# A graph layer on one core: turns of one pair of blocks instead of two, sums that lag, and a gate for every unit's gathers

## The chip, the core and the metric

One Trainium2 chip, one core of it. The core has TensorE (PE in the profile, with its weight loads as PEld), VectorE (DVE), ScalarE (ACT), GpSimd (POOL) and SyncE (SP); each works through its own instructions in order and waits for others by semaphores. DMA transfers are issued from the queues of SP, ACT and POOL. The metric is the device time of one execution in microseconds, as a median over runs.

## What is computed

A layer of a graph network over 6250 nodes of 256 features and 206250 edges, sorted by destination, all in float32. Cut to what matters:

```python
h = jnp.maximum(_layernorm(x), 0.0)
polarity = jnp.clip(edge_attr[:, 0:1], 0.0, 1.0)
raw = edge_attr[:, 1:]                                        # 64 features an edge
e = jax.nn.relu(raw @ W_e1.T + b_e1) @ W_e2.T + b_e2
edge_emb = (e * (polarity + 0.01)) @ W_le.T + b_le
msg = jax.nn.relu(h[src] + edge_emb)
aggr = jax.ops.segment_sum(msg, dst, num_segments=6250)
g = (h + aggr) @ W_g1.T + b_g1
g = layernorm(g) * ln_g + ln_b
out = x + jax.nn.relu(g) @ W_g2.T + b_g2
```

## The kernel before

**Layout of the work.** Edges come in tiles of 128; four tiles are a block (512 edges), half a block (two tiles, 256 edges) is a **unit**, and two blocks, so four units, are a **pair**. There are 403 blocks, 806 units (`NU`) and 202 pairs (`NP`). The two matrices after the first relu are multiplied into one in the prologue (`wc_s`), so an edge passes three stages of matmuls:

- **First layer** (`first_layer`, line 310), per pair: eight matmuls in the profile, 64 rows deep and 512 columns wide, two blocks at a time in the two halves of the array. Each of the four results fills a PSUM bank; three are evicted by ACT (line 327), one by DVE (line 324), with bias and relu, into `e1`. It runs two pairs ahead.
- **Edge products** (`edge_part`, line 347), per unit: eight matmuls of 128 x 128 weights and 256 columns into one bank. DVE evicts it with the bias into `msg` (line 353).
- **Sums** (`add_up`, line 740), per pair: 16 matmuls by a one-hot matrix `sel` of 128 x 32, four of them side by side in the array, which add the messages of a destination into `pd`.

Seven PSUM banks go round (`Ring`) among the first two stages and the node work; `pd` is the eighth. A bank is taken again when its reader, seven takings ago, has read it.

**Gathers and products.** Between the second and the third stage stands `whole(u)`: DVE multiplies `msg` by the polarity and adds the node rows `h[src]` (line 718, two instructions a unit), and ACT takes the relu (line 725). The node rows are fetched by POOL with two indirect DMAs a unit (`gather`, line 663) from `hb_d`, which the prologue writes. POOL has 1604 of these to issue and, from its first one on, nothing else. Their targets are 20 places in SBUF (`HG`), a place being free when the sums of the unit 20 before are done; the profile names the places `hx` and `hg`.

**Order.** The whole order is written out by the main loop over units `u` from `LEAD` = 22 on. Each turn of the loop makes the edge products of unit `u` (`forward`), then as many products `whole(made)` as fall due, then at most one piece of node work (`due`). The number of products due is `u + 1 - lag`, with a lag of 18 units at the start that falls by one every `SHRINK` = 44 units to 1 at the end (lines 978 and 979). So edges run ahead of products by up to 22 units, and the lead is used up over the run.

At `u % 4 == TURN` = 1 `forward` calls `turn_of(q)` for the pair `q = u // 4`. Between pairs `FEW` = 6 and 196 (`by_two`) this acts at even pairs alone, and for two pairs: first the sums of all pairs that are ready (`add_pairs`, line 772: those whose four products have been issued), then the first layers of pairs `q + 2` and `q + 3`, then the loads of raw features on SP. Outside that range it acts at each pair: first layer, then sums, then loads. In the unit before a turn by two, one product is held back until after the turn (the last term of `lag`).

**Gates.** Gathers are issued in step with PE. `paced` (that is `in_step`, line 676) is called behind every edge product and every half of a first layer with the planner's cost of it (`EDGE` 1.754, `LAYER` 0.9; sums add `SUMS` 0.46 a block and node steps `NODES` 0.81), which add up to `spent`. At two places in eight units (`gate`) it issues all gathers for which `(got - 2 * RAW) * STEP < spent + AFLOAT + HALF`, with `STEP` = 1.288 a gather, `AFLOAT` = 6.0 and `HALF` the cost of four units; the first of them waits for the PE instruction just made, the others follow it in POOL's order. A first call ahead of the loop lets the first gathers go without a wait. If a product is due whose gather is not yet issued, `gathers(made + 1)` issues it.

**Node work.** When the last group of sums that reaches a window of 128 nodes is done, `far_work` issues, over the following units, the read of the sums, two transposes (lines 174, 207), and the two products of the node's own layers (lines 189, 220) with their normalisation on DVE and ACT. `due` lets one such step go per unit, none in the unit before a turn by two and in the turn's own (`QUIET`, units 0 and 1 of every eight).

Of the kernel before, what the change touches and what calls it, by code (L numbers as in the profile page):

```python
# [36 lines left out]
NP = -(-NB // 2)  # L37
# [3 lines left out]
LEAD = 22  # L41
LEAST = 1
EDGE, LAYER, SUMS, NODES = 1.754, 0.9, 0.46, 0.81
STEP = 1.288
AFLOAT = 6.0
HALF = 4 * EDGE + 2 * LAYER + 2 * SUMS + NODES
BANKS = 7
SHRINK = 44
RAW = 4
HG = 16 + RAW  # L50
FEW = 6
QUIET = (0, 1)
TURN = 1
# [48 lines left out]
def gnn_kernel(ctx: ExitStack, tc: tile.TileContext, x, src_c, dst_c, dst_r, pol_c, raw_t, w_e1t, w_e2,  # L102
# [138 lines left out]
    NU = 2 * NB  # L241
    fast = ExitStack()
    fast.enter_context(tc.manual_schedule())
    with fast:
# [39 lines left out]
        def load_pair(q):  # L284
            if q >= NP:
                return
            t, k = divmod(q, 2)
            if k == 0:
                fours[t] = ld.tile([P, 2, 512], F32, name="raw")
            raw[q] = fours[t][:, k, :]  # L290
            if q < 4:
                nc.sync.dma_start(out=raw[q], in_=raw_t[t, :, k, :])
            elif k == 0:
                nc.sync.dma_start(out=fours[t], in_=raw_t[t])

        def first_layer(q):

            bs = [b for b in (2 * q, 2 * q + 1) if b < NB]
            if not bs:
                return  # L300
            for b in bs:
                e1[b] = features[b % 8]
            pe, z, readers = {}, {}, {}
            for c in range(2):
                olds = []
                for s, b in enumerate(bs):
                    pe[s, c] = ps().rearrange("p a b -> p (a b)")
                    olds.append(ps.old())
                for s, b in enumerate(bs):
                    z[c] = nc.tensor.matmul(pe[s, c], we1_s[s * F:(s + 1) * F, c * P:(c + 1) * P],  # L310
                                            raw[q][s * F:(s + 1) * F, :], start=True, stop=True)
                    ps.wrote(z[c], len(bs) - 1 - s)
                    reader, writer = olds[s]
                    readers[s, c] = reader
                    if reader is not None and writer is not None:
                        tc.declare_no_dep(z[c].ins, writer.ins, reason="the bank's reader has waited for it")
                    if s == 0:
                        for reader, _ in olds[1:]:
                            behind(z[c], reader)
                paced(LAYER, z[c], c == 0 and not (by_two(q - 2) and q % 2))  # L320
            for c in range(2):
                for s, b in enumerate(bs):
                    if s == c == 1:
                        a = nc.vector.tensor_scalar(e1[b][:, c, :], pe[s, c], be1_s[:, c:c + 1], 0.0, op0=ALU.add,  # L324
                                                    op1=ALU.max)
                    else:
                        a = nc.scalar.activation(e1[b][:, c, :], pe[s, c], AF.Relu, bias=be1_s[:, c:c + 1])  # L327
                    behind(a, z[c])
                    evictions[b, c] = a
                    apart_from(a, evictions.get((b - 8, c)), readers[s, c])  # L330
                    ps.read(a, len(bs) * (1 - c) + len(bs) - 1 - s)
            raw.pop(q)
# [5 lines left out]
        def edge_part(u):  # L338

            nonlocal last_z  # L340
            b, v = divmod(u, 2)
            pz = ps()
            before, _ = ps.old()
            for i in range(2):
                k = (2 * v + i) * P
                for c in range(2):
                    last_z = nc.tensor.matmul(pz[:, i, :], e1[b][:, c, k:k + P], wc_s[:, c, :], start=c == 0, stop=c == 1)  # L347
            ps.wrote(last_z)
            msg[u] = msg_p.tile([P, 2, D], F32, name="msg")
            if plain(u):  # L350
                a = nc.scalar.activation(msg[u], pz, AF.Copy)
            else:
                a = nc.vector.tensor_add(msg[u], pz, bc_s)  # L353
            ps.read(a)
            apart_from(a, before)
            if v == 1:
                e1.pop(b)
            paced(EDGE, last_z, by_two(u // 4) and u % 8 == 5)

        last_z = None  # L360
        sums = lambda last: None
        paced = lambda us, behind, gate=False: None

        def by_two(q):
            return FEW <= q < NP - FEW

        def turn_of(q):


            if not by_two(q):  # L370
                if q + 2 < NP:
                    first_layer(q + 2)
                sums(q == NP - 1)
                if q % 2 == 0:
                    load_pair(q + 4)
                    load_pair(q + 5)
            elif q % 2 == 0:
                sums(False)
                first_layer(q + 2)
                first_layer(q + 3)  # L380
                load_pair(q + 4)
                load_pair(q + 5)

        def forward(u):

            edge_part(u)
            if u % 4 == TURN:
                turn_of(u // 4)

        nc.vector.memset(eps_t, EPS)  # L390
# [42 lines left out]
        with tc.tile_pool(name="p1", bufs=4) as p1, tc.tile_pool(name="p1x", bufs=11) as p1x:  # L433
# [76 lines left out]
            for k in range(len(parts) + 1):  # L510
                last = len(parts) - 1
# [20 lines left out]
                for _ in range((k > 0) + (k > 2 and k % 3 > 0)):  # L532
                    u = next(units, None)
# [108 lines left out]
        with tc.tile_pool(name="hg", bufs=1) as hg_p, tc.tile_pool(name="ms", bufs=4) as ms_p, \  # L642
# [6 lines left out]
            got = 2 * RAW  # L649
            acc = {}  # L650
            done = {}
            made = 0
# [18 lines left out]
            def gathers(last):  # L671

                while got < 2 * min(NU, last):
                    gather()

            def in_step(us, behind, gate=False):

                nonlocal spent
                spent += us
                while gate and (got - 2 * RAW) * STEP < spent + AFLOAT + HALF and got < 2 * min(NU, 4 * summed + HG):  # L680
                    gather(behind)
                    behind = None

            def select(g):

# [86 lines left out]
            def add_pairs(last=False):  # L772

                nonlocal summed
                whole_groups = []
                pairs = 0
                while summed + pairs < NP and min(4 * (summed + pairs) + 4, NU) < made + last:
                    pairs += 1
                for _ in range(pairs):
                    newest = done.get(4 * summed + 3, ())  # L780
                    for b in (2 * summed, 2 * summed + 1):
                        if b < NB:
                            whole_groups.append(add_up(b, newest))
                            newest = ()
                            if b % L == 0 and group_of(b) + 2 < NG:
                                rest.extend(select(group_of(b) + 2))
                    summed += 1

                for g in whole_groups:
                    keep(g)  # L790
# [151 lines left out]
            def due():  # L942

                nonlocal spent
                fns = todo.pop(now, deque())
                if fns and not (by_two(now // 4) and now % 8 in QUIET):
                    spent += NODES
                    fns.popleft()()
                if fns:
                    todo.setdefault(now + 1, deque()).extendleft(reversed(fns))  # L950

            gathers(RAW + 1)
            sums = add_pairs
            paced = in_step
            in_step(0.0, None, True)
            def strips():
                rows_of_edges()
                rest.extend(select(0) + select(1))
# [12 lines left out]
            for u in range(LEAD, NU):  # L971
                now = u
                forward(u)

                if u >= NU - 24:
                    gathers(4 * summed + HG)

                lag = max(LEAST, LEAD - RAW - u // SHRINK) + (by_two(u // 4) and (u + 1) % 8 == TURN)
                ready_for = min(u + 1 - lag, 5 * (u + 1 - LEAD) // 4)
                between = piece  # L980
                while made < ready_for:
                    gathers(made + 1)
                    whole(made, between)
                    made += 1
                    between = lambda: None
                if between is piece:
                    piece()
                due()
                for fn in moves.pop(now, []):
                    fn()  # L990
                if len(rest) > 3:
                    piece()
                if u == NU - 24:
                    for w in range(NW):
                        if groups_of(w)[-1] == NG - 1:
                            late[w] = node_work(w, True)
                if u == LEAD + 60:
                    flag = nc.values_load(bad_i[0:1, 0:1], min_val=0, max_val=4 * P)
# [214 lines left out]
```

## Time and profile before

| | us |
|---|---|
| median of 3 runs | 2155.08 |
| lowest, highest | 2152.94, 2156.09 |
| the profiled execution, its own time | 2150.16 |
| its span from first to last instruction | 2148.4 |

The granted TensorE clock of the profiled execution is 0.996 of full speed. In a row of groups stand: line, engine, operation, tile written and tiles read, count, busy time and mean duration in ns, then the idle time just before these instructions and what ended it. A row of waits has the waiting group, the releaser, the summed wait, how often, and the longest. A row of the chain or of the timeline has start, duration and what ran; the chain is the run's last-ending work followed back, and where PE carries it, its pieces lie end to end. A row of a window has its bounds and length, then busy time and count of PE, PEld, DVE, ACT and POOL, the granted clock, DMA share and GB/s. fp32 matmuls overlap their neighbours, so a matmul's mean duration is longer than the distance between two of them.

### The profile page before, as it was taken

What the parts mean: (1) busy time and instruction counts of PE and PEld (TensorE: products, weight loads), DVE (VectorE), ACT (ScalarE), POOL (GpSimd) and SP (SyncE); (2) the same over time, 40 slices, a digit from 0 to 9 for tenths busy, and PEclk for the clock granted to TensorE, in tenths of its full rate; (3) what the DMA queues carried; (4) which work ended last, traced back from release to release, by engine and by line L of the source; (5) the groups of instructions that cost most, each with busy time, mean ns of one, the idle gap of its engine ahead of it and who ended that gap; (6) DMA issues with size and microseconds to landing.
All of it is one profiled execution on the core that took longest, in us unless ns stands there. A gap on an engine that the chain in (4) does not pass through costs nothing.

```text
span 2148.4 us, 33462 instructions
## 1 busy us (share of the span) xinstructions
PE 2104.8 (98%) x11940; PEld 1559.8 (73%) x11940; DVE 1594.2 (74%) x3455; ACT 1010.0 (47%) x1804; POOL 1621.4 (75%) x1675
## 2 busy tenths in 40 slices
PE   9999999999999999999999999999999999999998
PEld 6677776777777676777777776777777777777766
DVE  7888776877777777777777767776777777777776
ACT  7544444444444444444444444444544454444443
POOL 6777777777777777777777777777777777777775
PEclk9999999999999999999999999999999999999999
DMA  9544545455545444544454554455444455454543
GB/s 317 185 147 140 152 148 159 142 154 152 163 149 155 148 150 145 162 141 152 144 153 148 160 159 136 147 158 159 144 150 144 149 156 152 148 152 140 160 139 92
DMA packets 143638, 330.35 MB, mean 154 GB/s; under 512 B 35999, under 2 KB 71416, under 8 KB 142712
## 3 DMA queue, kind: packets, MB, share of 16 engines
q0 software_dynamic: 77376, 211.39, 34.2%
q1 hardware_dynamic: 64788, 113.47, 15.9%
q10 hardware_dynamic: 1300, 3.28, 0.4%
q8 instruction: 95, 1.56, 0.3%
q14 instruction: 79, 0.65, 0.1%
HBM read 306.24 MB, written 34.08 MB: 158 GB/s over the span
## 4 chain that ended last, share of the span: by engine, by line
PE 53%; POOL 26%; issue 11%; DMA 6%; DVE 3%; ACT 0%; SPq 0%; POOLq 0%; ACTq 0%; DVEq 0%
PE pz L347 35%; POOL hg L663 21%; PE pz L310 10%; POOL hx L663 5%; PE pd L740 4%; DMA hg<-hb_d,src_s 4%; PE pz L220 1%; DVE hg L718 1%; PE pz L189 1%; DMA raw<-in_raw_t_dram 1%; DVE msg L353 1%; DMA hx<-hb_d,src_s 1%; PE pz L207 0%; DVE st L159 0%; PE pz L174 0%
## 5 line engine op out<-in xcount | busy, mean ns | idle before, releaser
L663 POOL DMA_INDIRECT hg<-hb_d,src_s x1284 | 1259.7, 981 | 393.8 <-issue 368.6
L347 PE MATMUL pz<-wc_s,e 128*128 128x256 f32 x6448 | 1456.0, 382 | 2.1 <-DVE msg L353 2.1
L347 PEld LDWEIGHTS pz<-wc_s,e 128*128 128x128 f32 x6448 | 1212.0, 190 | 238.2 <-ACT e L327 74.1
L725 ACT ACTIVATE hg<-hg 128x512 f32<-128x512 f32 x641 | 404.2, 631 | 806.2 <-DVE hg L718 806.2
L718 DVE SCALAR_TENSOR_TENSOR hg<-msg,pol_s,hg 128x256 f32<-128x256 f32 x1284 | 591.4, 479 | 229.4 <-DMA hg<-hb_d,src_s 225.8
L353 DVE TENSOR_TENSOR msg<-pz,bc_s 128x512 f32<-128x512 f32 x799 | 542.3, 683 | 15.9 <-PE pz L347 15.2
L310 PE MATMUL pz<-raw,we_s 64*128 64x512 f32 x1612 | 384.0, 608 | 18.4 <-DVE msg L353 9.9
L663 POOL DMA_INDIRECT hx<-hb_d,src_s x320 | 316.8, 990 | 97.5 <-issue 92.9
L327 ACT ACTIVATE e<-pz,vecs 128x512 f32<-128x512 f32 x605 | 360.8, 693 | 60.3 <-PE pz L310 59.9
L324 DVE TENSOR_SCALAR e<-pz,vecs 128x512 f32<-128x512 f32 x201 | 150.6, 749 | 206.6 <-PE pz L310 206.2
L310 PEld LDWEIGHTS pz<-raw,we_s 64*128 64x128 f32 x1612 | 145.5, 187 | 211.1 <-issue 130.4
L725 ACT ACTIVATE hx<-hx 128x512 f32<-128x512 f32 x164 | 103.4, 631 | 195.1 <-DVE hx L718 195.1
L718 DVE SCALAR_TENSOR_TENSOR hx<-msg,pol_s,hx 128x256 f32<-128x256 f32 x328 | 151.8, 480 | 57.4 <-DMA hx<-hb_d,src_s 56.7
L740 PE MATMUL pd<-hg,sel 128*32 128x256 f32 x2560 | 160.4, 384 | 11.0 <-ACT hg L725 11.0
L740 PEld LDWEIGHTS pd<-hg,sel 128*32 128x32 f32 x2560 | 74.7, 110 | 82.0 <-issue 25.9
L694 DVE SCALAR_TENSOR_TENSOR sel<-iota_w,zero_c,rel 128x256 f32<-128x256 f32 x202 | 96.5, 478 | 0.0
L189 PE MATMUL pz<-wg_s,hT 128*128 128x256 f32 (+1 forms) x196 | 50.8, 382 | 0.8 <-ACT hT L178 0.8
L220 PE MATMUL pz<-wg_s,nT 128*128 128x256 f32 (+1 forms) x196 | 50.5, 380 | 0.9 <-ACT nT L211 0.9
L740 PE MATMUL pd<-hx,sel 128*32 128x256 f32 x656 | 43.5, 382 | 0.0
L189 PEld LDWEIGHTS pz<-wg_s,hT 128*128 128x128 f32 (+1 forms) x196 | 36.8, 190 | 7.6 <-ACT hT L178 1.2
L470 POOL TENSOR_TENSOR hb<-xt,rows_b 128x256 f32<-128x256 f32 (+1 forms) x49 | 34.1, 727 | 10.5 <-ACT e L327 3.5
L220 PEld LDWEIGHTS pz<-wg_s,nT 128*128 128x128 f32 (+1 forms) x196 | 37.0, 190 | 6.6 <-ACT nT L211 1.1
(113 smaller groups left out, 518.0 us busy)
## 6 DMA issues: line engine op xcount, KB each, us to landing
raw<-in_raw_t_dram SPq DMA_DIRECT2D x99, 512.0 KB
hg<-hb_d,src_s POOLq DMA_INDIRECT x1284
sum_d<-zero_d SPq DMA_DIRECT2D x47, 256.0 KB
ab<-sum_d SPq DMA_DIRECT2D x47, 256.0 KB
sum_d<-ms SPq DMA_DIRECT2D x264, 32.0 KB
hb_d<-hb SPq DMA_DIRECT2D x12, 512.0 KB
xt<-in_x_dram SPq DMA_DIRECT2D x48, 128.0 KB
out_dram<-ot SPq DMA_DIRECT2D x48, 128.0 KB
```

The costliest lines, as they stand in the source:

```text
L189: z = nc.tensor.matmul(ph[:n, 0, :], aT[:, c, :n], wg1_s[:, c, :], start=c == 0 and not bias_by_pe, stop=c == 1)
L220: z = nc.tensor.matmul(po[:n, 0, :], nT[:, c, :n], wg2_s[:, c, :], start=c == 0, stop=c == 1)
L310: z[c] = nc.tensor.matmul(pe[s, c], we1_s[s * F:(s + 1) * F, c * P:(c + 1) * P], raw[q][s * F:(s + 1) * F, :], start=True, stop=True)
L324: a = nc.vector.tensor_scalar(e1[b][:, c, :], pe[s, c], be1_s[:, c:c + 1], 0.0, op0=ALU.add, op1=ALU.max)
L327: a = nc.scalar.activation(e1[b][:, c, :], pe[s, c], AF.Relu, bias=be1_s[:, c:c + 1])
L347: last_z = nc.tensor.matmul(pz[:, i, :], e1[b][:, c, k:k + P], wc_s[:, c, :], start=c == 0, stop=c == 1)
L353: a = nc.vector.tensor_add(msg[u], pz, bc_s)
L663: g = nc.gpsimd.indirect_dma_start(out=hg[u][:, i, :], out_offset=None, in_=hb_d, in_offset=bass.IndirectOffsetOnAxis(ap=src_s[:, 2 * u + ...
L694: nc.vector.scalar_tensor_tensor(sel[g][:, k * S:k * S + n, :], iota_w.rearrange("p (o w) -> p o w", o=1).to_broadcast([P, n, W]), zero_c, ...
L718: product = nc.vector.scalar_tensor_tensor(hg[u][:, i, :], m[:, i, :], pol_s[:, 2 * u + i:2 * u + i + 1], hg[u][:, i, :], op0=ALU.mult, op ...
L725: done[u] = product, nc.scalar.activation(hg[u], hg[u], AF.Relu)
L740: z = nc.tensor.matmul(acc[g][j * W:(j + 1) * W, :], sel[g][:, k * S + j, :], m[:, j % 2, :], start=k == 0, stop=b == blocks_of(g)[-1])
```

## The change

Five things, in the code of one function each:

1. `turn_of`: every pair has its own turn, over the whole run: first layer of pair `q + 2`, then the sums, then the loads at even pairs. The hold-back of a product in the unit before a turn goes with it, from every eighth unit to every fourth.
2. `add_pairs`: a pair is summed only when its last unit lies `LATER` = 3 units further behind the products issued (not at the end of the run), and the product made early in the turn does not count.
3. `forward` calls `ahead` (`one_ahead`) before the turn: one product, with its relu, is issued ahead of the turn's first layer, and so ahead of its evictions on DVE and ACT.
4. `in_step`: every call is a gate, for one unit (two gathers) at most, of which the first waits for the PE instruction; `HALF` is gone from the condition, and so is the call that let the first gathers go ahead of the loop.
5. `due`: node steps keep out of units 0 and 1 of every four (`now % 4`), again the unit before a turn and the turn's own.

```diff
-                paced(LAYER, z[c], c == 0 and not (by_two(q - 2) and q % 2))
+                paced(LAYER, z[c])
...
-            paced(EDGE, last_z, by_two(u // 4) and u % 8 == 5)
+            paced(EDGE, last_z)
...
         def turn_of(q):
-            if not by_two(q):
-                if q + 2 < NP:
-                    first_layer(q + 2)
-                sums(q == NP - 1)
-                if q % 2 == 0:
-                    load_pair(q + 4)
-                    load_pair(q + 5)
-            elif q % 2 == 0:
-                sums(False)
+            if q + 2 < NP:
                 first_layer(q + 2)
-                first_layer(q + 3)
+            sums(q == NP - 1)
+            if q % 2 == 0:
                 load_pair(q + 4)
                 load_pair(q + 5)
...
             if u % 4 == TURN:
+                ahead(u)
                 turn_of(u // 4)
...
-            def in_step(us, behind, gate=False):
+            def in_step(us, behind):
                 nonlocal spent
                 spent += us
-                while gate and (got - 2 * RAW) * STEP < spent + AFLOAT + HALF and got < 2 * min(NU, 4 * summed + HG):
+                if got % 2 == 0 and (got - 2 * RAW) * STEP < spent + AFLOAT and got < 2 * min(NU, 4 * summed + HG):
                     gather(behind)
-                    behind = None
+                    gather()
...
-                while summed + pairs < NP and min(4 * (summed + pairs) + 4, NU) < made + last:
+                while summed + pairs < NP and min(4 * (summed + pairs) + 4, NU) < made - eager + last - (0 if last or summed > NP - 2 * FEW else LATER):
                     pairs += 1
...
-                if fns and not (by_two(now // 4) and now % 8 in QUIET):
+                if fns and not (by_two(now // 4) and now % 4 in QUIET):
...
+            def one_ahead(u):
+                nonlocal made, eager
+                eager = by_two(u // 4) and made + 1 < due_at(u)
+                if eager:
+                    gathers(made + 1)
+                    whole(made, piece)
+                    made += 1
+
+            def due_at(u):
+                lag = max(LEAST, LEAD - RAW - u // SHRINK) + (by_two(u // 4) and (u + 1) % 4 == TURN)
+                return min(u + 1 - lag, 5 * (u + 1 - LEAD) // 4)
...
-            in_step(0.0, None, True)
...
-                lag = max(LEAST, LEAD - RAW - u // SHRINK) + (by_two(u // 4) and (u + 1) % 8 == TURN)
-                ready_for = min(u + 1 - lag, 5 * (u + 1 - LEAD) // 4)
+                ready_for = due_at(u)
```

More of the change, by code (lines that the diff above doesn't have):

```diff
@@ L45 @@
 AFLOAT = 6.0
-HALF = 4 * EDGE + 2 * LAYER + 2 * SUMS + NODES
+LATER = 3
 BANKS = 7
@@ L357, in edge_part @@
                 e1.pop(b)
-            paced(EDGE, last_z, by_two(u // 4) and u % 8 == 5)
+            paced(EDGE, last_z)
         last_z = None
         sums = lambda last: None
-        paced = lambda us, behind, gate=False: None
+        ahead = lambda u: None
+        paced = lambda us, behind: None
         def by_two(q):
@@ L952, in gnn_kernel @@
             gathers(RAW + 1)
+            def one_ahead(u):
[8 more added lines that the diff above has]
+                return min(u + 1 - lag, 5 * (u + 1 - LEAD) // 4)
+            eager = False
             sums = add_pairs
+            ahead = one_ahead
             paced = in_step
-            in_step(0.0, None, True)
             def strips():
```

## Prediction

> **What bounds the kernel now.** I read the page first: busy shares, chain, costliest groups.
>
> ```profile
> PE 2104.8 (98%) x11940; PEld 1559.8 (73%) x11940; DVE 1594.2 (74%) x3455; ACT 1010.0 (47%) x1804; POOL 1621.4 (75%) x1675
> ...
> PE 53%; POOL 26%; issue 11%; DMA 6%; DVE 3%; ACT 0%; SPq 0%; POOLq 0%; ACTq 0%; DVEq 0%
> ```
>
> PE looks full and POOL three-quarters full, yet the chain runs through POOL and its "issue" for 37%. So I asked for POOL alone: a window over its gathers, its first and last rows, and its waits.
>
> ```profile
> 65.00:2130.00 2065.00, 1576.53 (x1604) 1.00 0.50 150
> ```
> ```profile
> 64.99 0.98 POOL L663 DMA_INDIRECT hg<-hb_d,src_s  x1 [2.88 <-DVE st L159]
> 66.27 0.95 POOL L663 DMA_INDIRECT hg<-hb_d,src_s  x1 [0.30 <-issue]
> ```
> ```profile
> 2128.96 0.94 POOL L663 DMA_INDIRECT hg<-hb_d,src_s  x1 [0.30 <-issue]
> ```
> ```profile
> POOL hg L663 <- issue: 368.6, 1210, 0.3
> ...
> POOL hg L663 <- PE pz L310: 6.4, 21, 0.3
> ```
>
> From 65 to 2130 us POOL issues 1604 gathers (two per unit), each preceded by 0.30 us and never by more: the longest wait is 0.3, and a gather released by PE pays the same 0.3. So it never rests: 2065 / 1604 = 1.287 us a gather, 2.575 us a unit, and gathers alone reach 2130 of 2148.4 us. **POOL is saturated.** Then what is PE? Chain pieces, where PE carries them, give the bare lengths:
>
> ```profile
> 1000.25 1.86 PE pd L740 x32
> 1002.12 3.63 PE pz L310 x16
> 1005.75 14.01 PE pz L347 x64
> 1019.76 1.86 PE pd L740 x32
> ...
> 1027.18 0.22 PE pz L174 x2
> ...
> 1032.59 0.86 PE pz L189 x4
> ```
>
> One cycle of eight units, sums (L740), first layers (L310) and edge products (L347), is 1.86 + 3.63 + 14.01 = 19.50 us, gapless. Node work comes on top: 0.22 for a transposition, 0.86 for a product. How much of the run is more than that? The stretch in which turns go by two, by PE's lines:
>
> ```profile
> 98.40:2050.40 1952.00, 1927.16 (x11037) 1430.37 (x11037) 1447.66 (x3072) 908.92 (x1607) 1489.34 (x1519) 1.00 0.50 151
> ```
> ```profile
> L310 PE MATMUL pz<-raw,we_s 64*128 64x512 f32 x1488 | 352.2, 608 | 13.1 <-DVE msg L353 8.5 <-DVE e L324 4.2 <-ACT e L327 0.3
> L740 PE MATMUL pd<-hg,sel 128*32 128x256 f32 x2434 | 152.6, 384 | 11.0 <-ACT hg L725 11.0
> L189 PE MATMUL pz<-wg_s,hT 128*128 128x256 f32 x180 | 46.3, 380 | 0.8 <-ACT hT L178 0.8
> L220 PE MATMUL pz<-wg_s,nT 128*128 128x256 f32 x176 | 45.2, 379 | 0.0
> L740 PE MATMUL pd<-hx,sel 128*32 128x256 f32 x624 | 41.3, 382 | 0.0
> L174 PE MATMUL pz<-ident,stb 128*128 128x128 f32 x90 | 17.2, 273 | 0.0
> L207 PE MATMUL pz<-ident,hs 128*128 128x128 f32 x88 | 16.8, 273 | 0.0
> ```
>
> 1488 / 16 = 93 cycles, 1813.5 us. Node work: (180 + 176) / 4 x 0.86 + (90 + 88) / 2 x 0.22 = 96. L740 has 3058 matmuls where 93 cycles need 2976: five pairs of sums more, 5 x 0.93 = 5. Together 1914.5, so 37.5 of the 1952 us are PE standing still or stretched. The releasers say for what: banks not yet evicted by DVE, sums whose rows ACT has not finished. Both queue behind DVE products, and what DVE waits for longest in all is
>
> ```profile
> DVE hg L718 <- DMA hg<-hb_d,src_s: 225.8, 290, 3.6
> ```
>
> the landing of a gather. So PE's losses are POOL's lateness, handed on.
>
> **The change part by part.** *Turns of one pair.* Turns at 95 even pairs become turns at 190 pairs (pairs 6 to 195). PE does the same matmuls but goes round L347, L310, L740 twice as often. The end of the old kernel, where turns already go by one and the first layer stands first, shows the price:
>
> ```profile
> 2072.50 5.42 DMA hx<-hb_d,src_s
> ...
> 2079.08 7.13 PE pz L347 x24
> 2086.22 1.92 PE pz L310 x8
> 2088.13 1.00 PE pd L740 x16
> 2089.14 1.06 PE pz L189 x4
> 2090.20 6.91 PE pz L347 x32
> 2097.10 1.92 PE pz L310 x8
> ```
>
> 2097.10 - 2086.22 = 10.88, less the four L189 (0.86): 10.02 us for four units, 20.04 for eight, against 19.50. Each extra turn costs 0.54 us of PE time; 95 x 0.54 = **+51.3 us**. It is a drain at each change of matmul shape: a sum's or first layer's entry shows up as 1.92 + 1.92 for what took 3.63, 1.00 + 1.00 for 1.86. Nothing can cover it, because it is PE's own time.
>
> *What it wins back* is at most the 37.5 us above and one more loss near the end, where a gather's landing (2072.50, 5.42) holds PE up:
>
> ```profile
> 2079.08 7.13 PE L347 MATMUL pz<-wc_s,e 128*128 128x256 f32 x24 [2.11 <-DVE msg L353]
> ```
> ```profile
> 2050.00:2130.00 80.00, 77.89 (x460) 56.34 (x459) 59.96 (x136) 34.71 (x63) 61.02 (x63) 0.98 0.48 137
> ```
>
> 2.1 us of waiting, and then 24 matmuls take 7.13 us where 32 take 6.91, 1.9 us more than their share; the granted clock of this stretch is 0.98 instead of 1.00. 37.5 + 4 = 41.5. Does it come back? Units are consumed faster than edges are made: the lag falls by one every SHRINK = 44 units, so 45 units of gathers fall to 44 of edges. PE's unit was 19.50 / 8 + 96 / 744 = 2.567 us, so gathers were wanted every 2.567 x 44 / 45 = 2.510 us, against 2.575 that POOL manages: 0.065 short on each of some 750 units, 49 us, of which 41.5 became stalls and the rest was POOL's initial lead. With turns by one, PE's unit is 20.04 / 8 + 0.129 = 2.634, the demand every 2.575 us: **supply and demand meet**. So nearly all stalls go, but because PE got slower. What stays is unevenness: cycles with and without node work, and a tight start. Bounds: 0 (all goes) to 41.5 (none); I take 4, a tenth, near the lower end since the mean shortage is gone.
>
> *Lagging sums* (LATER = 3) let the newest unit summed lie five or more units behind the newest product, so the 11.0 us of L740 for ACT are among what goes. It delays freeing the 20 places; 8 or more units (over 20 us) stay between product and gather limit. No cost.
>
> *One unit's products ahead of its evictions.* DVE does two L718 before the turn's eviction instead of after; the counts are unchanged. Price if the gather is late: DVE and ACT reach the evictions late. With four banks to a turn instead of eight, seven banks leave an eviction two edge units and a turn, 2 x 1.73 (6.91 / 4) + 2.92 (2089.14 - 2086.22) = 6.4 us. I take zero; the bound is the 41.5 of before.
>
> *Gates per unit.* About 780 gathers get a wait on PE, against some 190 gates now. Behind a waiting gather stand all later gathers (POOL has nothing else after 65 us), and behind them DVE's products. An open gate costs nothing beyond the 0.3 (rows above). A late one is not in the trace: nothing at the low end, 780 x 0.3 = 234 us at the far end if each restart showed its lead once more. I take zero, the row being at that end. Can they be late? A unit u may be gathered once (2u - 8) x 1.288 < `spent` + 6, so at `spent` = 2.576u - 16.3. `spent` grows by 9.74 a pair and 0.81 a node step, near 10.5 for four units, so the gate lies at about edge unit 15.8 + 0.975u, and the product, by the lag, at 17.6 + 0.978u: 1.8 units or 4.7 us later. Thirteen start-up steps, counted 0.81 each, open gates 10.5 us earlier, the lagging sums some 5 us later: 10 us in all between gate and use, once the start is over. Two gathers and the slow landing above take 1.3 + 5.4 = 6.7. And the gates' pace: real PE time is 10.02 + 0.52 = 10.54 a pair, so they open every 1.288 x 10.54 / 10.5 = 1.293 us a gather, a hair slower than POOL's 1.287: POOL is tied to PE and cannot run off. The free run of eleven gathers at the start goes, but it was early:
>
> ```profile
> L718 DVE SCALAR_TENSOR_TENSOR hg<-msg,pol_s,hg x1284: 464/478/553, 85.9 to 2132.8; 128x256 f32<-128x256 f32 x184
> ```
>
> the first product that reads gathered rows of `hb_d` stands at 85.9 us, 19 us after the first two gathers.
>
> *Rest:* node steps in half of the units instead of three-quarters (200 steps in 784 units: enough), same loads on SP, every second pair, same sums out.
>
> **Sum**, against the profiled execution: 2148.4 - 41.5 + 51.3 + 4 = 2162.2 us of span. What lies around the span was 1.8 us (2150.16 in all): 2164.0. The median of the three runs, 2155.08, stands 4.9 above that execution; with PE as the bound instead of POOL I carry half: **2166 us**, 0.5% slower.
>
> **A rule that speaks against it.** The Trainium skill (Perfetto Trace Analysis, section Identifying the Most-Contended Engine) says that matmul busy time misleads because matmuls are pipelined, and that weight-load busy time is the better gauge. By its gauge PE stands at 73%, not 98%, and has room for the 51 us, so POOL would stay the bound. The trace does not agree here: the cycle of 19.50 us repeats gapless, and the one-pair turn has already shown its 0.54.
>
> **Rivals.** *PE has room (not slower).* If PE's switches disappear into its queue of weight loads once fewer waits stand between them, the end stays POOL's: 65 + 2065 + 18.4 = 2148.4, the median 2155; within 0.2%. It decides if an extra turn costs less than 41.5 / 95 = 0.44 us instead of 0.54. For it: weight loads are busy only 73%. Against: the rows from 2086 on, without any wait in them, cost 10.02 each. Faster needs in addition shorter gathers.
>
> *The gates hold POOL.* At the start PE itself stands still:
>
> ```profile
> 78.26 1.13 PE L310 MATMUL pz<-raw,we_s 64*128 64x512 f32 x4 [1.39 <-DVE msg L353]
> ```
>
> Gates behind it are late, POOL loses some microseconds and, with supply equal to demand, does not regain them; each later stall of PE delays gates in the same way. Another 8 to 18 us, median 2174 to 2184. It decides if the 10 us between gate and use are not there. Against: 6.7 us is what a unit needs.
>
> *The stalls stay.* If DVE's waits for landings, not POOL's rate, make them, 2148.4 + 51.3 + 6.7 gives a median near 2206.
>
> **How the numbers follow.** Forecast 0.68 (2156 to 2174, from no stall left to 12 us); PE has room 0.13, 0.02 of it faster; gates hold POOL 0.12; stalls stay 0.07. About 0.2% is what a measurement here can tell from no change: 2150.8 to 2159.4. The forecast's lowest edge lies inside it, 0.03 of its chance. So faster 0.02, same 0.14, slower 0.84. The range leaves out the first and the last rival: 2156 to 2184.
>
> **What would show it.** Right: cycles of L310, L740, 32 x L347 of 10.02 us repeating; PE's waits on L310 and L740 nearly gone; some POOL waits on PE over 0.3; the last gather well before the last L347. Wrong: gathers still back to back to the end (POOL still the bound), or cycles longer than 10.02 with DVE waiting for landings (gates too late), or extra turns under 0.44 us.

## The result, and the profile after

| | before | after |
|---|---|---|
| median, us | 2154.54 (6 runs) | 2164.41 (6 runs) |
| lowest, highest | 2152.94, 2157.14 | 2163.36, 2169.94 |
| the profiled execution, own time | 2150.16 | 2163.58 |
| its span | 2148.4 | 2161.8 |

After over before is 1.0049, with a 95% interval of 1.0037 to 1.0061: 0.5% slower, where 2166 was forecast. The span was forecast as 2162.2. Here and below, ratios leave out the executions at a much lower granted clock, one of the kernel before at 2424 us (0.85) and one of its variants at 4049 us (0.79).

The page of the kernel after, its row of busy engines and the head of its chain:

```profile
PE 2144.2 (99%) x11940; PEld 1538.4 (71%) x11940; DVE 1606.0 (74%) x3455; ACT 985.0 (46%) x1804; POOL 1625.3 (75%) x1675
...
PE 95%; DVE 1%; DMA 1%; issue 1%; POOL 1%; ACT 0%; DVEq 0%; SPq 0%; ACTq 0%; POOLq 0%
```

The busy shares say nearly nothing: POOL has the same 75%, PE one point more. The chain says more: PE carries 95% of the span instead of 53%, POOL and "issue" 2% instead of 37%. The chain between 1000 and 1031 us (start, length, what):

```profile
1010.11 1.92 PE pz L310 x8
1012.03 1.00 PE pd L734 x16
1013.03 7.11 PE pz L347 x32
1020.14 1.92 PE pz L310 x8
1022.05 1.00 PE pd L734 x16
1023.06 7.10 PE pz L347 x32
1030.16 1.92 PE pz L310 x8
```

From L310 to L310 it is 10.03 and 10.02 us, the forecast's cycle. Of the 191 cycles that begin with a turn (186 with one pair summed, five with two), all but a handful near the start have this length to 0.01 us once node work is subtracted, or 10.89 where two pairs are summed.

PE's two largest rows of waits, and those rows of its groups that held stalls before (count, busy, mean ns, then idle time and what ended it):

```profile
PE pz L347 <- DVE msg L353: 4.6, 3, 2.2
PE pz L310 <- DMA raw<-in_raw_t_dram: 1.7, 1, 1.7
```
```profile
L310 PE MATMUL pz<-raw,we_s 64*128 64x512 f32 x1612 | 402.3, 616 | 1.7 <-DMA raw<-in_raw_t_dram 1.7
L734 PE MATMUL pd<-hg,sel 128*32 128x256 f32 x2560 | 171.1, 385 | 0.0
```

Over the whole run the first layer's idle time fell from 18.4 us (13.1 in the stretch that the prediction shows) to 1.7, that of the sums from 11.0 to nothing. DVE's longest-lasting row of before, the wait for a gather's landing, went from 225.8 us to

```profile
DVE hg L712 <- DMA hg<-hb_d,src_s: 30.4, 41, 2.5
```

So nearly all rows came in time. POOL, however, worked as hard as before. A window from its first gather to the end of its last, the first gathers, and two rows of its waits:

```profile
64.16:2135.65 2071.49, 2065.74 (x11561) 1480.86 (x11561) 1544.59 (x3259) 932.71 (x1695) 1580.48 (x1604) 1.00 0.50 149
```
```profile
64.16 0.98 POOL L657 DMA_INDIRECT hg<-hb_d,src_s  x1 [2.42 <-DVE mv L160]
65.44 0.95 POOL L657 DMA_INDIRECT hg<-hb_d,src_s  x1 [0.30 <-issue]
68.70 1.52 POOL L657 DMA_INDIRECT hg<-hb_d,src_s  x1 [2.31 <-PE pz L347]
```
```profile
POOL hg L657 <- PE pz L347: 34.4, 105, 2.3
POOL hg L657 <- PE pz L310: 9.3, 30, 0.4
```

1604 gathers in 2071.5 us are 1.291 us each, against 1.287. Only three gaps between gathers are longer than 0.4 us (2.31, 0.41 and 0.67), and one of them, the first gate at 68.70, holds nearly all that the new gates cost POOL. What changed is who is last. The chain at the end of the run:

```profile
2135.69 5.18 PE pz L347 x24
2140.87 1.86 PE pd L734 x32
```

The last gather ends at 2135.65, and 5.2 us of edge products still follow. Before, the last edge products ended at 2127.63 and POOL's last gather only at 2129.9. What follows the last gather took 18.5 us before and takes 26.2 now. Both engines are full; PE now ends last, by little.

### The profile page after: what moved, and what is told of

It is laid out like the page before. It is cut to its first block, busy times and chain, and to the rows that moved or that the text cites. A ratio compares the mean times of both kernels' runs of the same rounds, so it can differ in the third digit from the quotient of the medians.

```text
span 2161.8 us, 34047 instructions
## 1 busy us (share of the span) xinstructions
PE 2144.2 (99%) x11940; PEld 1538.4 (71%) x11940; DVE 1606.0 (74%) x3455; ACT 985.0 (46%) x1804; POOL 1625.3 (75%) x1675
## 4 chain that ended last, share of the span: by engine, by line
PE 95%; DVE 1%; DMA 1%; issue 1%; POOL 1%; ACT 0%; DVEq 0%; SPq 0%; ACTq 0%; POOLq 0%
PE pz L347 64%; PE pz L310 17%; PE pd L734 9%; PE pz L189 2%; PE pz L220 2%; POOL hg L657 1%; DMA raw<-in_raw_t_dram 1%; PE pz L207 1%; PE pz L174 0%; DMA hg<-hb_d,src_s 0%; DVE msg L353 0%; ACT xt L460 0%; DMA we_s<-in_w_e_dram 0%; DVE hg L712 0%; DVE hx L712 0%
## 5 line engine op out<-in xcount | busy, mean ns | idle before, releaser
L347 PE MATMUL pz<-wc_s,e 128*128 128x256 f32 x6448 | 1479.6, 383 | 5.7 <-DVE msg L353 4.6
L347 PEld LDWEIGHTS pz<-wc_s,e 128*128 128x128 f32 x6448 | 1204.5, 190 | 240.5 <-DVE e L324 40.3
L353 DVE TENSOR_TENSOR msg<-pz,bc_s 128x512 f32<-128x512 f32 x799 | 549.3, 688 | 404.3 <-PE pz L347 395.2
L712 DVE SCALAR_TENSOR_TENSOR hg<-msg,pol_s,hg 128x256 f32<-128x256 f32 x1284 | 582.0, 478 | 31.3 <-DMA hg<-hb_d,src_s 30.4
L310 PE MATMUL pz<-raw,we_s 64*128 64x512 f32 x1612 | 402.3, 616 | 1.7 <-DMA raw<-in_raw_t_dram 1.7
L327 ACT ACTIVATE e<-pz,vecs 128x512 f32<-128x512 f32 x605 | 368.3, 678 | 10.3 <-PE pz L310 10.3
L310 PEld LDWEIGHTS pz<-raw,we_s 64*128 64x128 f32 x1612 | 139.7, 187 | 163.8 <-issue 135.5
L734 PE MATMUL pd<-hg,sel 128*32 128x256 f32 x2560 | 171.1, 385 | 0.0
L734 PEld LDWEIGHTS pd<-hg,sel 128*32 128x32 f32 x2560 | 67.6, 109 | 144.7 <-issue 116.6
L189 PE MATMUL pz<-wg_s,hT 128*128 128x256 f32 (+1 forms) x196 | 50.7, 382 | 0.0
L734 PEld LDWEIGHTS pd<-hx,sel 128*32 128x32 f32 x656 | 17.2, 109 | 37.6 <-issue 29.6
```

What stands on the lines that cost most here:

```text
L189: z = nc.tensor.matmul(ph[:n, 0, :], aT[:, c, :n], wg1_s[:, c, :], start=c == 0 and not bias_by_pe, stop=c == 1)
L712: product = nc.vector.scalar_tensor_tensor(hg[u][:, i, :], m[:, i, :], pol_s[:, 2 * u + i:2 * u + i + 1], hg[u][:, i, :], op0=ALU.mult, op ...
L734: z = nc.tensor.matmul(acc[g][j * W:(j + 1) * W, :], sel[g][:, k * S + j, :], m[:, j % 2, :], start=k == 0, stop=b == blocks_of(g)[-1])
```

## The experiments

Ratios are to the kernel before, run beside the variant on the same chip. Theory A is that of the prediction: before, POOL's supply of gathers sets the pace and PE's stalls are its lateness; after, PE's own cycle of 10.02 us does, and the rest of the change costs next to nothing. Its rivals: the gates hold POOL, or the other parts of the change make part of the time.

### The turns by themselves

On before, `turn_of` alone becomes that of after:

```diff
-            if not by_two(q): ...
-            elif q % 2 == 0:
-                sums(False)
+            if q + 2 < NP:
                 first_layer(q + 2)
-                first_layer(q + 3)
+            sums(q == NP - 1)
+            if q % 2 == 0:
                 load_pair(q + 4)
                 load_pair(q + 5)
```

> The kernel before with turns of one pair alone; sums without the extra lag, no product ahead of the turn, the old gates. Theory A (the stalls were POOL's shortage of 0.065 us a unit, and go because PE's unit grows by 0.067 us): cycles of L310, L740 and 32 x L347 of 10.02 us as in the whole change, span 2158 to 2166 us, ratio to before 1.004 to 1.008. Theory B (the lagging sums, the product ahead and the gates took the stalls away): the stalls of 41 us stay beside 51 us of extra turns, span 2185 to 2199 us, ratio 1.017 to 1.024.

Measured 2158.82 us, ratio 1.0031 (1.0018 to 1.0043), span 2157.9: just under both of Theory A's ranges, and far from Theory B's. PE's longest wait, in sum, and a stretch of the chain:

```profile
PE pz L310 <- DVE msg L353: 2.1, 2, 1.5
```
```profile
1001.43 7.10 PE pz L347 x32
1008.54 1.92 PE pz L310 x8
1010.45 1.00 PE pd L733 x16
1011.46 7.10 PE pz L347 x32
1018.56 1.92 PE pz L310 x8
```

The stalls are gone here too, with the old gates, no lag and no product ahead: turns of one pair alone drive them out. That fits the prediction, by which a PE that needs its rows later isn't short of them. But such a turn is also smaller, with four first-layer banks to evict at a time instead of eight while seven go round, and that could spare PE the same waits. This run can't tell the two apart; the next but one does, for the old turns.

Its span is also 3.9 us shorter than that of the whole change (the two ratios' intervals just overlap), and the traces show where most of it lies. The sums of two pairs fall together in 25 turns of this kernel and in five of after: two turns then take 9.02 + 10.89 = 19.91 us instead of 20.04, and 20 x 0.13 = 2.6 us. The lag is not what parts the pairs again, for after without it (below) has five such turns too. By the code it is the hold-back of a product ahead of a turn. With it in every eighth unit, as here, the products done grow by five units and by three from turn to turn, and while the lag between edges and products is 16, 12, 8 or 4 units, two pairs become ready at every second turn; with it in every fourth unit they grow by four each time, and one pair does. The trace agrees: 24 of the 25 turns stand at such units. The rest lies in stalls near the start, which differ from one execution to the next.

### The gates by themselves

```diff
-                while gate and (got - 2 * RAW) * STEP < spent + AFLOAT + HALF and ...
+                if got % 2 == 0 and (got - 2 * RAW) * STEP < spent + AFLOAT and ...
                     gather(behind)
-                    behind = None
+                    gather()
...
-            in_step(0.0, None, True)
```

> The kernel before with the gates per unit alone: one unit of gathers at every call, no free run at the start; turns of two pairs as before. Theory A: POOL stays saturated and sets the end; it loses the 1 to 6 us by which its first gathers wait for PE, and PE's stalls stay near 40 us: span 2148 to 2156 us, ratio 1.000 to 1.004. Theory B (the gates took the stalls away): PE's summed waits for DVE and ACT fall below 10 us and the span below 2140 us.

Measured 2152.29 us, ratio 1.0001 (0.9990 to 1.0013); the profiled span of 2145.9 lies a little under what was expected, that of the median execution (2150.5) inside it. PE stalls as before:

```profile
PE pd L740 <- ACT hg L725: 10.7, 5, 3.9
PE pz L310 <- DVE msg L353: 8.0, 8, 2.0
```

A gate for each unit neither costs nor cures anything in this kernel, so the gates aren't what removed the stalls in after. The rest of the change as a whole, on turns of two pairs, was not tried.

### Fewer gathers, before and after

In both kernels one gather in sixteen from unit 40 on is left out, 95 of 1604; those rows of `hg` keep what was in them.

```diff
+                if u >= 40 and u % 8 == 7 and i == 1:
+                    return
                 g = nc.gpsimd.indirect_dma_start(
```

> The kernel before without the second gather of every eighth unit from unit 47 on (95 of 1604 gathers, 5.9%; the rows of these tiles are left out of the messages). Theory A: gathers are then supplied every 2.42 us a unit where 2.51 is wanted, so PE's 41 us of stalls go and PE sets the end: span 2105 to 2115 us, ratio 0.979 to 0.984. Theory B (PE's stalls come from the order of turns, not from POOL's rate): span above 2135 us.

> The changed kernel without the same 95 gathers (their rows are left out of the messages). Theory A: PE sets the end already, so nearly nothing is gained: span 2156 to 2162 us, ratio to the kernel before 1.003 to 1.006, and the difference to the kernel before with the same gathers left out is the price of 95 extra turns alone, 51 us (49 to 54). Rival (POOL, still issuing back to back, shares the bound): a gain of 10 us or more.

Before without them: 2114.66 us, ratio 0.9822 (0.9809 to 0.9836). After without them: 2162.24 us, ratio to before 1.0048 (1.0034 to 1.0061), where after itself has 1.0049. The profiled spans, 2116.6 and 2162.5, lie just above what was expected. The same relief on POOL is worth 38 us in one kernel and nothing in the other. In the first, POOL now waits for PE; two rows of its waits, the start of an old cycle of the chain, and a long window of all engines in the kernel before and, below it, in this variant:

```profile
POOL hg L665 <- PE pz L310: 49.8, 56, 2.7
POOL hg L665 <- PE pz L347: 30.6, 38, 1.2
```
```profile
1011.74 1.86 PE pd L742 x32
1013.60 3.63 PE pz L310 x16
1017.24 1.92 PE pz L347 x8
```
```profile
260.00:2010.00 1750.00, 1727.85 (x9907) 1284.69 (x9909) 1289.32 (x2740) 814.83 (x1444) 1335.26 (x1362) 1.00 0.50 150
260.00:2010.00 1750.00, 1750.00 (x10077) 1308.43 (x10076) 1295.70 (x2787) 836.96 (x1471) 1286.65 (x1307) 1.00 0.49 147
```

Without the 95 gathers PE works for all of these 1750.00 us, where before it stood still for 22. The turns are the old ones of two pairs with their eight banks, so it was the supply of gathered rows that made the stalls of before, not the size of a turn. That smaller turns had no part in driving them out, in after and in the turns alone, is argued from this and not tested: a slower PE with turns of two pairs was not run.

POOL waits in the second too, for the same reason:

```profile
POOL hg L659 <- PE pz L347: 122.4, 167, 2.4
```

This pair is the cleanest measurement of what the change costs PE, since POOL bounds neither: 2162.24 - 2114.66 = 47.6 us, or 45.9 by the spans. 51 was expected (49 to 54), so it missed by little. The cycles differ as they should, 19.51 against 2 x 10.02, so 0.53 x 95 = 50.4. The rest lies ahead of 351 us: by then the edge products of the before-variant stand 5.2 us behind those of before, and those of the after-variant 0.9 behind those of after, and 50.4 - 4.3 is 46.1.

### The other parts, undone one by one in after

No lag of the sums, no product ahead of the turn, the old gates with their free run at the start:

```diff
-LATER = 3
+LATER = 0
```
```diff
-                eager = by_two(u // 4) and made + 1 < due_at(u)
+                eager = False
```
```diff
-                if got % 2 == 0 and (got - 2 * RAW) * STEP < spent + AFLOAT and ...
+                while gate and (got - 2 * RAW) * STEP < spent + AFLOAT + HALF and ...
                     gather(behind)
-                    gather()
+                    behind = None
...
+            in_step(0.0, None, True)
```

> The changed kernel with LATER = 0: sums are issued as soon as their products are. Theory A: supply and demand of gathers meet, so a product is rarely late; PE's waits on L734 for ACT come back by 0 to 6 us: span 2161 to 2168 us. Theory B (the lag is what removed the stalls): 20 us or more of waits on L734, span above 2178 us.

> The changed kernel with no product issued ahead of the turn. Theory A: evictions have 6.4 us of room either way; span 2159 to 2165 us, as the whole change within 0.2%. Theory B: PE waits on L310 and L347 for DVE and ACT return, span above 2175 us.

> The changed kernel with the old gates: two in eight units, each for up to four units of gathers, and the free run at the start. Theory A: POOL issues back to back either way; it gains the 2 to 5 us lost at the start, which PE's bound hides: span 2158 to 2164 us. Theory B (gates per unit keep products on time): span above 2175 us.

| undone | median, us | ratio to before | span |
|---|---|---|---|
| lag of the sums | 2162.55 | 1.0048 (1.0034 to 1.0062) | 2159.9 |
| product ahead of the turn | 2163.13 | 1.0047 (1.0033 to 1.0060) | 2161.3 |
| gates per unit | 2161.91 | 1.0044 (1.0030 to 1.0057) | 2159.7 |

None of the three can be told from after's 1.0049; the span without the lag lies 1 us under what was expected. Once turns go by one, PE has next to no wait left that a lag, an earlier product or finer gates could shorten. The hold-back in every fourth unit and the node steps' units weren't undone by themselves.

### The order within a turn

In after, sums ahead of the first layer:

```diff
+            sums(q == NP - 1)
             if q + 2 < NP:
                 first_layer(q + 2)
-            sums(q == NP - 1)
```

> The changed kernel with the sums ahead of the first layer in every turn. Theory A: the turn has the same three changes of matmul shape, so the cycle stays at 10.02 us; span 2159 to 2166 us. Theory B (the first layer ahead spares PE a wait, or the price hangs on the order of shapes): the cycle differs from 10.02 by more than 0.05 us or stalls of over 10 us in all appear.

Measured 2167.17 us, ratio 1.0072 (1.0058 to 1.0086), span 2163.1, as expected. The cycles are 10.02 as in after. The two ratios stand 0.0023 apart, some 5 us, and their intervals just overlap. In the profiled execution the order cost PE nothing: its last edge products ended at 2140.7, in after at 2140.9. But the last gather ended at 2144.8 instead of 2135.65, behind them, because the gathers themselves took longer (1590.4 us in all against 1580.5), and the run ended 18.3 us after it, as before's does. So in after POOL is only some microseconds from ending last again. Why its gathers were longer, and whether that holds for the slower executions, is open.

### Moving the gathers earlier

If POOL bounds before, more of its gathers done in the prologue should bring the end forward. `RAW` is the number of units whose rows are fetched there, in the idle time of POOL; the number of places stays 20, and the prologue's buffers give up the room:

```diff
-RAW = 4
-HG = 16 + RAW
+RAW = 6
+HG = 20
...
-AHEAD = 10
+AHEAD = 9
...
-tc.tile_pool(name="p1x", bufs=11) as p1x
+tc.tile_pool(name="p1x", bufs=10) as p1x
```

(and 8, 8 and 9 in the second of them.)

> The kernel before with six instead of four units gathered straight from x in the prologue (RAW 6, one chunk of rows fewer loaded ahead, still 20 places): four gathers leave the saturated stretch for a time when POOL waits anyway. Theory A (POOL's stretch sets the end of the kernel before): 4 x 1.287 = 5.1 us less if the prologue does not grow, span 2142 to 2148 us, ratio 0.996 to 0.999. Rival (PE's own order sets the end): no change or slower by what the prologue grows.

> The same with eight units (RAW 8, two chunks of rows fewer ahead). Theory A: up to 8 x 1.287 = 10.3 us less, span 2137 to 2148 us, ratio 0.994 to 0.999; less if the eight more gathers in front of the node rows push the prologue back. Rival: no change or slower.

Both missed: 2153.00 us, ratio 1.0006 (0.9996 to 1.0016), and 2167.65 us, 1.0071 (1.0058 to 1.0084). By time alone this fits the rival as well as Theory A. The traces show what happened. POOL's first gather from `hb_d` and its longest waits, first with 6 units, then with 8:

```profile
66.94 0.98 POOL L663 DMA_INDIRECT hg<-hb_d,src_s  x1 [2.65 <-DVE mv L160]
```
```profile
POOL hx L663 <- PE pz L310: 6.5, 6, 5.0
```
```profile
70.83 0.98 POOL L663 DMA_INDIRECT hg<-hb_d,src_s  x1 [2.83 <-DVE st L159]
...
106.18 1.03 POOL L663 DMA_INDIRECT hg<-hb_d,src_s  x1 [5.52 <-PE pz L347]
```
```profile
POOL hx L663 <- PE pz L310: 11.4, 5, 10.2
```

The prologue ends later (gathers start 1.95 and 5.8 us later than at 64.99), and around 105 us POOL waits at its gates for a PE that has fallen behind: 5.0 us with 6, 5.5 and 10.2 with 8. With 8, for instance, 5.8 + 5.2 + 9.9 (the waits beyond the usual 0.3) less 8 gathers x 1.287 is 10.6 us; the last gather ended 13.0 us later than before (2142.9 against 2129.9), and the span was 12.6 longer. The other 2.4 us are gathers that took a little longer. With 6, the last one ended 4.6 us later, and the span was 4.2 longer. So the expected gain was lost at the start. In both, the run ended 18.1 us after the last gather, in before 18.5. PE's last edge products started only 1.9 and 10.7 us later than in before, after 13.5 and 26.9 at 351 us: PE caught up, and the end of the run kept to the gathers. That speaks for Theory A on before, in these profiled executions; that gathers moved forward at no cost would gain time is not shown by them.

### One more visit to the sums

The price of one more change of matmul shape and back: in after, the two blocks of a pair are summed at two places in 172 pairs, the second two units later. Same matmuls, 172 more visits.

```diff
+                        if b % 2 and i == pairs - 1 and FEW <= summed < NP - 4 * FEW:
+                            second.append(b)
+                            break
...
                 forward(u)
+                if second and u % 4 == 3:
+                    second_block()
```

> The changed kernel with the two blocks of a pair summed at two places, one in the turn and one two units later, for 172 pairs: the same matmuls, one more visit to L734 between edge products. Theory A (a turn's price is the change of matmul shape, twice per visit; the last cycles of the kernel before, with sums but no first layer, show 8.11 us for 32 x L347 and 16 sums whose bare lengths are 6.91 and 0.86, so 0.34 us a visit): 172 x 0.34 = 58 us more than the changed kernel, span 2212 to 2228 us, ratio 1.028 to 1.035. Rival (the price is waits around the first layer): under 15 us more.

Measured 2218.70 us, ratio 1.0308 (1.0292 to 1.0324), span 2216.5: 54.3 us above after by the medians, 54.7 by the spans, so 54.5 / 172 = 0.32 us a visit. That is in Theory A's range and far from the rival's. Its chain shows where that sits:

```profile
1016.36 0.57 PE pd L734 x8
1016.93 1.92 PE pz L347 x8
1018.85 0.86 PE pz L189 x4
1019.72 1.73 PE pz L347 x8
1021.44 0.57 PE pd L734 x8
1022.01 3.65 PE pz L347 x16
```

Two visits of 0.57 us stand for one of 1.00, 0.14 more; and the first eight edge products after each take 1.92 where those after the node's product L189, which has their shape, take 1.73. 0.14 + 0.19 = 0.33. No wait stands between these pieces. It is PE's own time, as the prediction had it for the extra turn.

## Why the prediction was right, point by point

**What bounded before.** POOL, as argued from its gapless gathers against the 98% of PE. Shown by taking 95 gathers away, which took 38 us off; the two variants whose gathers ended later agree, but don't decide it. The prediction's reading that DVE's and ACT's lateness was POOL's, handed on, is shown by the same run: with the instructions of DVE and ACT and the order of turns as they were, PE's waits for them are gone from 260 to 2010 us.

**+51.3 us for 95 extra turns.** Measured 0.53 us a turn in the cycles, 50.4 in all, and 46 to 48 between the two variants in which POOL doesn't bound. The chains show its parts: two first layers at two places take 2 x 1.92 us instead of 3.63, two sums 2 x 1.00 instead of 1.86, and 64 edge products in two runs 2 x 7.10 instead of 14.01: 0.21 + 0.14 + 0.19 = 0.54. The split sums give 0.32 us for a visit to the sums alone, with the last two of these parts. The Trainium skill (TensorEngine Tiling (Array Packing), section Key Properties) says that a change of the tiling mode drains TensorE; it gives no price. The traces agree, in that each change costs 0.14 to 0.21 us.

**-41.5 us of stalls, 4 of them left.** In after, the cycles that stand out between 98 and 2050 us are one of 14.01 us at 160.5 and two with 0.3 us each: 4.0 + 0.6 = 4.6. The two small ones hold two little matmuls each of the start-up work (L627, L632), which before has too and which the 41.5 took in as stalls. That the 4 came out is luck: the prediction chose a tenth between bounds of 0 and 41.5, for cycles with and without node work and a tight start. The cycles with node work came out as regular as those without; it is one event near the start, and in the variants with such turns the cycle there is too long by 0.8 to 3.7 us. Its rows are the ones of the timeline around 161 us:

```profile
160.88 0.48 DVE L712 SCALAR_TENSOR_TENSOR hg<-msg,pol_s,hg 128x256 f32<-128x256 f32 x1 [2.52 <-DMA hg<-hb_d,src_s]
161.28 1.82 DVE L606 TENSOR_REDUCE ends<-rel 128x1 f32<-128x1612 f32 x1
...
163.02 0.68 DVE L353 TENSOR_TENSOR msg<-pz,bc_s 128x512 f32<-128x512 f32 x1
...
163.75 3.68 PE L347 MATMUL pz<-wc_s,e 128*128 128x256 f32 x8 [2.23 <-DVE msg L353]
```

A product waits 2.52 us for its gather; a reduction of 1.82 us from the start-up work comes next on DVE; the eviction stands behind both, and PE behind the eviction. This is the price named for products that stand ahead of evictions, "if the gather is late", and it was due once. Without that edit a cycle there is still 2.19 us too long, with a wait of PE for DVE of 1.41 us at 161.7, so the edit isn't its only cause.

Put together: -41.5 + 50.4 + 4.6 = +13.5 us of span, and measured 2161.8 - 2148.4 = 13.4.

**Supply and demand meet.** Right: gathers every 1.291 us, and nothing gained in after from fewer of them. But the text offered "gathers still back to back to the end" as the sign that POOL was still the bound, and that sign is there: POOL never rests in after either. That sign tells nothing. When two engines are brought to the same pace both look saturated, and only the order at the end (5.2 us between the last gather and the last edge product) and a run that relieves one of them tell which one counts. "The last gather well before the last L347" was too much said as well, and of POOL's waits over 0.3 us there were three.

**Gates, lag, product ahead: zero each.** None of these edits undone gave a difference that can be measured. Against the turns alone, the rest of the change together cost some 4 us of span, mostly because pairs are no longer summed by twos, and by the code that is the hold-back in every fourth unit. The prediction had no such term: it counted "same sums out".

**From span to median.** The prediction carried half of the 4.9 us by which before's median stood above its profiled execution. After's median lies 0.8 above its own. From 2164.0 to 2166 it had allowed 2.0, so 1.2 too much, and that is most of the 1.6 us between 2166 and 2164.41.

**The rivals.** PE has no room: its cycles are gapless at 99%, with weight loads busy for 71%, and taking gathers from POOL won nothing. The rule weighed there from the Trainium skill (Perfetto Trace Analysis, section Identifying the Most-Contended Engine) therefore doesn't hold here; by that gauge PE would have had 29% of its time free. The gates held POOL for 2.0 us once and for under 0.5 us twice more, not for 8 to 18. And the stalls didn't stay.

## What to carry to other kernels

When an engine stalls on two others, ask what those wait for: here DVE and ACT were only passing on POOL's gathers, and while POOL issues without a rest, a cure at DVE or ACT has little to win. A slower cycle on the bottleneck's customer can remove its stalls without a gain; count the price of the cycle against the stalls before calling their absence progress. And when both engines come out full, take some work from one of them and look whether the end moves.

## What the runs showed of the hardware

- **Behind some stalls of PE the granted clock halves, behind others not.** After the wait of 2.23 us above, eight edge products took 3.68 us, and the cycle lost 4.0. The windows of the wait and of what follows it (length, busy times, then the granted clock, DMA share, GB/s), and the same place in the variant with the sums first:

```profile
160.45:163.86 3.41, 1.18 (x19) 0.53 (x17) 2.98 (x4) 0.63 (x1) 2.78 (x3) 1.00 0.51 166
163.86:167.27 3.41, 3.41 (x9) 2.59 (x10) 3.41 (x9) 0.63 (x1) 2.51 (x3) 0.50 0.27 79
```
```profile
163.85 1.99 PE L347 MATMUL pz<-wc_s,e 128*128 128x256 f32 x8 [2.21 <-DVE msg L353]
```

  The granted clock is 0.50 for 3.41 us behind the stall, then 1.00 again. Ahead of its end, the kernel before has four such stretches, all of 3.41 us, at 82.6, 833.5, 1635.6 and 2079.4 us; the last is the prediction's event, 2.1 us of wait and 1.9 more behind it. The one at 1635.6 follows two shorter waits, of 0.95 and 1.24 us. But the wait of 2.21 us in the last row above, and one of 2.29 us at 368 in the kernel before, have none behind them, and the eight products took 1.99 us: the length of a wait alone doesn't decide, and what else does is open. The Trainium skill (TensorE: Matmul & The Clock Gate, Part 1: The HAM clock gate) has the clock drop to half after an idle window of about 3.4 us; by these rows less idle time than that can be enough. In the variant with 8 prologue units the start-up had the same in large:

```profile
80.00:100.00 20.00, 16.99 (x47) 9.78 (x46) 15.94 (x29) 13.40 (x26) 16.04 (x14) 0.67 0.31 89
```

  a clock of 0.67 over 20 us, and behind it the gates for which POOL waited.
- **More semaphore instructions cost POOL nothing here.** After gives POOL 837 of them where before has 253. The spaces between gathers sum to 491.0 us against 488.4, and the three long ones account for the difference; all others stay at about 0.30 us.
